# Sums in column streams, the order of two products, an earlier regrouping, and reciprocals in pieces, in a kernel of two attention layers

## The chip, the cores and the metric

The kernel runs on one core of a Trainium2 chip. Its engines work side by side, each through its own list of instructions in order: TensorE (PE) multiplies matrices, VectorE (DVE), ScalarE (ACT) and GpSimd (POOL) work on elements, and SyncE (SP) issues most transfers (DMAs). They wait for one another through semaphores. Matrix products land in PSUM, everything else lies in SBUF or in the chip's main memory. The metric is the time of one execution on the device in microseconds (us), as a median of runs. A profiled execution is a run of its own, with its own time.

## What is computed

The input is x, eight images of 512 channels and 32 x 32 = 1,024 tokens, all in f32. Two layers follow one another; each is `x = x + layer(groupnorm(x))`. Cut to what matters here:

```python
# layer 0, 8 heads of 64 channels; n = groupnorm of its input once more
q, k, v = split(qkv_w @ n + qkv_b)
a       = softmax(q.T @ k / 8) @ v          # per image and head, 1,024 x 1,024
out     = proj_w @ (n_in + a) + proj_b

# layer 1
q, k, v = w_q @ y, w_k @ y, w_v @ y
s       = einsum('gh,hqt->gqt', w_head, q.T @ k / 8)   # mixes the 8 heads
p       = softmax(s)
p       = (p - mean(p)) / sqrt(var(p) + eps) * gamma + beta   # per image and head
out     = (p @ v) as [tokens, channels] @ w_proj.T + b_proj
```

The softmax of both layers is done without its division: the kernel keeps exp(s), sums it over the keys, and multiplies the result of the values by the reciprocal of that sum.

## The kernel before

The order of every engine's instructions is the order of the program text; there is no planner. An `Agenda` holds small pieces of work under slot numbers, and the main loops call `run(slot)` at fixed places.

**Layer 0** goes image by image. The projections of q, k, v and the output each are seven products of half size in place of eight (`project0`). The attention of an image (`attention0`) is a loop over 64 steps: 8 groups (a pair of heads and half of the queries, 512 of them) times 8 blocks of 128 keys. A step has `scores` (four 64-row, 64-column matmuls in the four quadrants of the array, and then exp on ACT into a tile `e` of 128 x 2 x 512), and, one round later, `values` (four quadrant matmuls) and `sums` (DVE adds the `e` tiles of a group into `zacc`). When a group is through, the agenda gets three pieces of it: `totals` two steps on, `reciprocals` six on, `finish` ten on.

`totals` sums `zacc` over its partitions with a matmul by ones. Before, that is done in quadrants: for each half `a` of the partitions and each head `m` of the pair one matmul of 512 queries; the two halves lie in two PSUM tiles, ACT copies one into `row` and DVE the other, and two small DMAs spread a row over 128 partitions (`zc`). `reciprocals` adds the halves (`zs`), takes the reciprocal, and sends it through main memory (`zd`) to be broadcast over the partitions again (`rzb`); `finish` multiplies and adds into `xa`. In seven of the eight images the totals of the fifth group are followed on PE by a matmul of the next image's group statistics (L620), which waits for a small DVE copy (L618); and the totals of an image's last group come after the next image's k projection. In the last image nothing stands between them and the output projection.

**Layer 1** again goes image by image. `Projection` forms k, q and the output by seven products of quarters: `products` (eight matmul records of 512 columns each) and `leave` (what ACT or DVE does with the result). `run` takes them in `ORDER`. Products 3 and 4 are the last two: product 3 ends the quarter (0, 1), that is channels 0 to 255 and the later tokens; product 4 ends (1, 0), channels 256 to 511 and the earlier tokens. The k projections of all images but the first are placed by hand in the loop instead.

`Attention1` has 37 half-steps x. In `half_step(x)`, `scores` makes two score tiles (two of the four pairs of heads: pairs 0 and 1 when x is even, 2 and 3 when it is odd), which DVE or ACT copies to `raw`. A pair of half-steps fills the block t = x // 2 of `raw`. `regroup` then turns the block round with eight DMAs of 256 KB, r = 0 to 7, into one of the two halves of the buffer `re`, so that the heads lie along the partitions. Four half-steps after its scores, `mix` multiplies the block by the head weights (64 matmul records a mix, taken in `R_ORDER`), with exp on ACT; `squares`, `sum_e`, `sum_e2` and `values` follow one half-step later. In the steady state every mix and every values issues one regrouping DMA behind it. At the start (x up to 4) there is nothing to put them behind, and after the scores of x=1 and of x=3 all eight are issued at once.

`v_pair(b, i)` makes two blocks of 128 rows of v: sixteen matmul records, then one copy on ACT and one on DVE. Two of the four pairs of an image are made before its attention, two inside it. The weights of v lie in half of `re` at that time, in the space that the regrouping DMAs r = 0 to 3 of t=1 will write.

Every eight half-steps (a quarter `qb` of the queries) end with `totals(qb)`; two half-steps later `reciprocals` runs. It puts the broadcasts of `rzb` at the head of a list of pieces (`pieces`: also the loads of the next image and of weights), and `scores` sends one piece each time, behind its last matmul. `divide` multiplies by `rzb` six half-steps after the totals. For the last quarter of an image the broadcasts are issued at once.

PSUM has three tiles for scores, mixes and projections of layer 1 (`m_psum`), taken in turn; a matmul waits until the tile three back has been read.

Of the kernel before, what the change touches and what calls it, by code (L numbers as in the profile page):

```python
# [9 lines left out]
F32 = mybir.dt.float32  # L10
# [8 lines left out]
P = 128  # L19
# [448 lines left out]
def tile_two_attention_layers(  # L468
# [19 lines left out]
    nc = tc.nc  # L488
    B, C, T = x_d.shape
    H = w_head.shape[0]  # L490
    D = C // H
    NCC = C // P
    NT = T // P
    FB = 512
# [36 lines left out]
    ones = const_tile("ones", [P, P])  # L531
# [118 lines left out]
    with ExitStack() as l0:  # L650
# [9 lines left out]
        def small_psum(nm):  # L660
            return ps_a.tile([P, FB], F32, tag="small", name=nm)
# [308 lines left out]
        def attention0(b, agenda):  # L970
# [49 lines left out]

            def totals(g):

                z = [
                    ps_a.tile([P, FB], F32, tag="a0", name=f"z_{b}_{g}", bufs=2),
                    small_psum(f"z_{b}_{g}_1"),
                ]
                for a in range(2):
                    rows = slice(a * D, a * D + D)
                    for m in range(2):
                        nc.tensor.matmul(  # L1030
                            z[a][m * D : m * D + D], ones[rows, :D], zacc[g][rows, m],
                            start=True, stop=True,
                        )
                row = zpool.tile([P, 2, FB], F32, tag="row", name=f"row0_{b}_{g}", bufs=1)
                nc.scalar.copy(row[:, 0], z[0])
                nc.vector.tensor_copy(row[:, 1], z[1])
                zc[g] = stat.tile([P, 2, T // P], F32, tag="zc", name=f"zc_{b}_{g}")
                for a in range(2):
                    nc.sync.dma_start(out=zc[g][:, a], in_=row[0::D, a])

            def reciprocals(g):

                nc.vector.tensor_add(u[g][0], u[g][0], u[g][1])
                zs = stat.tile([P, T // P], F32, tag="zs", name=f"zs_{b}_{g}")
                nc.vector.tensor_add(zs, zc[g][:, 0], zc[g][:, 1])
                rz = stat.tile([P, T // P], F32, tag="rz0", name=f"rz_{b}_{g}")
                nc.vector.reciprocal(rz, zs)
                zd = dram.tile([2, FB], F32, tag=f"zd0_{b}_{g}", name=f"zd0_{b}_{g}")
# [100 lines left out]
    with ExitStack() as l1:  # L1149
# [144 lines left out]
                nc.vector.tensor_sub(t[:, i], x, y)  # L1294

        class Projection:
            ORDER = (1, 6, 2, 7, 5, 4, 3)

            def __init__(self, nm, key, n, t, finish, begin=None):

# [85 lines left out]
        def v_pair(b, i):  # L1386

            if i == 0:
                v_t[b] = kvpool.tile([P, NT, C], F32, tag="v", name=f"v1_{b}")
            ps = m_psum(f"pv1_{b}_{i}")  # L1390
            w = w_t["v", b]
            for m in range(2):
                for c in range(NCC):
                    nc.tensor.matmul(  # L1394
                        ps[:, m], y_t[b][:, c, ts(2 * i + m, P)], w[:, c],
                        start=(c == 0), stop=(c == NCC - 1),
                    )
            nc.scalar.copy(v_t[b][:, 2 * i], ps[:, 0])  # L1398
            nc.vector.tensor_copy(v_t[b][:, 2 * i + 1], ps[:, 1])  # L1399
# [158 lines left out]
        class Attention1:  # L1558
# [5 lines left out]
            def scores(self, x, i):  # L1564
# [15 lines left out]
                if x > MLAG:  # L1580
                    self.piece(last)
                if x % 2 and i == 1:
                    self.due = [(t, r) for r in R_ORDER]
                if x % 2 == 0 and i == 0:
                    self.raw[t] = rawpool.tile([P, H, 2, KB], F32, tag="raw", name=f"raw_{b}_{t}")
                dst = self.raw[t][:, 2 * hp : 2 * hp + 2]
# [133 lines left out]
            def reciprocals(self, qb, ag=None, x=None):  # L1720
# [7 lines left out]
                self.rzb = zpool.tile([P, T], F32, tag="rzb", name=f"rzb_{b}_{qb}")  # L1728
                rzb = self.rzb
                spread = [  # L1730
                    lambda two=two: nc.sync.dma_start(
                        out=rzb[two * D : two * D + D], in_=zd[two].partition_broadcast(D)
                    )
                    for two in range(2)
                ]
                if ag is None:
                    for fn in spread:
# [58 lines left out]
            def half_step(self, x, ag):  # L1796
# [23 lines left out]
                    self.scores(x, 1)  # L1820
                if 0 <= y < NX:
                    self.mix(y, 1)
                if x <= MLAG or x >= NX:
                    self.regroup(n=NR)
                if x >= NX:
# [28 lines left out]
        for b in range(B):  # L1854
            more = b + 1 < B
            a = Attention1(b)
            ag = Agenda()
            for i in range(NV):
                ag.at(1 + i, lambda i=i: v_pair(b, NV + i))
            free = (NX // 2 - 2 + b) % 2  # L1860
            if more:
                a.pieces += [lambda i=i: y_piece(b + 1, i) for i in range(4 * NCC)]
# [119 lines left out]
```

## Time and profile before

| what | value |
|---|---|
| median of 3 runs | 4345.27 us (4342.4 to 4345.67) |
| the profiled execution | 4355.81 us |
| its span, first to last instruction | 4353.9 us |
| TensorE clock granted | 0.995 of full speed |
| busy, share of the span: PE, DVE, ACT | 96%, 67%, 54% |
| one group's `totals` matmuls in layer 0 (64 groups) | 67.1 us busy in all |
| regrouping DMAs of 256 KB in layer 1 | 1,024 |
| broadcasts `rzb` in layer 1 | 64 of 256 KB |

In a line of a group, the first numbers are the busy time of all its instructions and the mean time of one in ns; behind the second bar stands how long the engine sat idle just before them, and what ended that. "64*64" is rows by columns of the array that a matmul takes up; each f32 matmul of the program gives two records. Matmuls overlap, so a record's length is longer than the distance to the next one. In a timeline the first number is the start in us from the span's start and the second the duration; in square brackets stands the idle time before. "issue" means that the engine waited for nothing that the profile shows. Idle time of an engine that isn't the bottleneck costs nothing.

### The profile page before, as it was taken

Reading aid. Unit: us, or ns where it says so; the run is one execution under the profiler, and the core shown is the slowest. Engines: PE = TensorE matmul, PEld = TensorE weight load, DVE = VectorE, ACT = ScalarE, POOL = GpSimd, SP = SyncE. Lnnn points to the kernel's source line nnn. Section 1 sums busy time; section 2 is a strip of 40 time slices with the busy share of each in tenths; the row PEclk is TensorE's granted clock in tenths of the full one; section 3 lists DMA queues with packets and bytes.
Section 4 is the critical chain, followed back from the end, with each engine's and each line's share of the span. In section 5 each row is a group of like instructions: output and inputs, shape, how many; then the busy total and the mean of one; then the engine's idle time right before and its main releaser. Section 6 shows DMA issues by size and latency. Waiting matters only on the chain.

```text
span 4353.9 us, 131477 instructions
## 1 busy us (share of the span) xinstructions
PE 4192.3 (96%) x58568; PEld 2243.2 (52%) x58568; DVE 2911.7 (67%) x3881; ACT 2329.9 (54%) x2730; POOL 53.3 (1%) x86
## 2 busy tenths in 40 slices
PE   7999999999999999799999999999999999999998
PEld 4353535353535353356466466466466466465565
DVE  4748484848484848458668668568577578577577
ACT  1717171717171716158368278277187287286385
POOL 0000000000000000000000000000000000000000
PEclk9999999999999999899999999999999999999999
DMA  4213131212121211257367377277286286375474
GB/s 145 77 54 101 50 104 49 79 49 79 52 76 54 74 49 43 87 140 191 123 166 183 105 187 180 97 195 189 81 202 172 90 206 158 114 199 141 135 175 136
DMA packets 260464, 521.21 MB, mean 120 GB/s; under 512 B 58992, under 2 KB 66544, under 8 KB 253232
## 3 DMA queue, kind: packets, MB, share of 16 engines
q1 hardware_dynamic: 255008, 509.92, 41.8%
q8 instruction: 461, 7.55, 0.8%
q0 software_dynamic: 2576, 0.69, 0.3%
q10 hardware_dynamic: 2304, 2.10, 0.2%
q14 instruction: 115, 0.94, 0.1%
HBM read 196.11 MB, written 46.92 MB: 56 GB/s over the span
## 4 chain that ended last, share of the span: by engine, by line
PE 84%; DVE 6%; DMA 5%; ACT 2%; issue 2%; SPq 1%; POOL 0%; DVEq 0%; ACTq 0%; POOLq 0%
PE a L1669 11%; PE s L1575 11%; PE m L1623 10%; PE s L982 8%; PE a L1008 8%; PE pk L1319 5%; PE pq L1319 4%; PE pp_p L856 4%; PE pv_p L856 4%; PE pv L1394 4%; PE pk_p L856 4%; PE pq_p L856 4%; PE pp L1319 3%; DMA re<-raw 2%; PE t L1700 2%
## 5 line engine op out<-in xcount | busy, mean ns | idle before, releaser
L1623 PEld LDWEIGHTS m<-wmix,re 64*64 64x64 f32 x32768 | 585.4, 135 | 141.9 <-issue 73.7
L1623 PE MATMUL m<-wmix,re 64*64 64x64 f32 x32768 | 602.1, 219 | 44.0 <-issue 34.9
L987 ACT ACTIVATE e<-s 128x1024 f32<-128x1024 f32 x512 | 497.4, 1026 | 235.4 <-PE s L982 235.4
L1629 ACT ACTIVATE e<-m 128x1024 f32<-128x1024 f32 x512 | 528.2, 1032 | 157.7 <-PE m L1623 154.2
L1647 DVE TENSOR_TENSOR z<-z,e 128x1024 f32<-128x1024 f32 x448 | 538.9, 1218 | 69.8 <-ACT e L1629 69.6
L1651 DVE TENSOR_TENSOR z<-z,e 128x1024 f32<-128x1024 f32 x448 | 534.9, 1219 | 74.6 <-ACT e L1640 74.4
L1669 PE MATMUL a<-e,v 128*64 128x256 f32 x4096 | 558.2, 392 | 27.5 <-ACT q L1691 20.9
L1575 PE MATMUL s<-k,q 64*64 64x256 f32 x8192 | 558.4, 388 | 6.2 <-DVE q L1431 4.6
L1590 ACT COPY raw<-s 128x1024 f32<-128x1024 f32 x368 | 372.7, 1015 | 284.4 <-PE s L1575 245.8
L982 PE MATMUL s<-q,k 64*64 64x512 f32 x4096 | 491.5, 594 | 2.3 <-ACT e L987 2.3
L995 DVE TENSOR_TENSOR zacc<-zacc,e 128x1024 f32<-128x1024 f32 x384 | 468.2, 1219 | 28.6 <-ACT e L987 3.9
L1008 PE MATMUL a<-e,v 64*64 64x512 f32 x4096 | 485.0, 589 | 0.0
L1640 ACT ACTIVATE e<-e 128x1024 f32<-128x1024 f32 x448 | 462.1, 1063 | 0.0
L1575 PEld LDWEIGHTS s<-k,q 64*64 64x64 f32 x8192 | 271.5, 132 | 274.5 <-issue 170.7
L1669 PEld LDWEIGHTS a<-e,v 128*64 128x64 f32 x4096 | 250.6, 136 | 155.0 <-issue 24.9
L1008 PEld LDWEIGHTS a<-e,v 64*64 64x64 f32 x4096 | 159.9, 133 | 281.2 <-issue 281.2
L982 PEld LDWEIGHTS s<-q,k 64*64 64x64 f32 x4096 | 156.2, 133 | 281.5 <-issue 257.7
L1588 DVE COPY raw<-s 128x1024 f32<-128x1024 f32 x144 | 176.1, 1223 | 96.3 <-PE s L1575 84.7
L1394 PE MATMUL pv<-re,y 128*128 128x512 f32 x512 | 227.6, 598 | 0.0
L1394 PEld LDWEIGHTS pv<-re,y 128*128 128x128 f32 x512 | 94.8, 190 | 120.1 <-issue 120.1
L1399 DVE COPY v<-pv 128x512 f32<-128x512 f32 x32 | 22.1, 689 | 149.4 <-ACT v L1398 149.4
L856 PE MATMUL pv_p<-left_v,tmp 128*128 128x256 f32 x512 | 115.1, 383 | 4.2 <-DVE tmp L885 4.2
(285 smaller groups left out, 4133.0 us busy)
## 6 DMA issues: line engine op xcount, KB each, us to landing
re<-raw SPq DMA_DIRECT2D x1024, 256.0 KB
left_q<-left_q SPq DMA_DIRECT2D x17, 1792.0 KB
left_p<-left_p SPq DMA_DIRECT2D x17, 1792.0 KB
left_k<-left_k SPq DMA_DIRECT2D x10, 1792.0 KB
x<-in_x_dram SPq DMA_DIRECT2D x32, 512.0 KB
rzb<-zd SPq DMA_DIRECT2D x128, 128.0 KB
x<-x SPq DMA_DIRECT2D x64, 256.0 KB
rzb<-zd SPq DMA_DIRECT2D x64, 256.0 KB
```

What stands on the lines that cost most here:

```text
L856: nc.tensor.matmul(out, st, mv, start=start, stop=(k == 1), skip_group_check=True)
L982: nc.tensor.matmul(ps[c * D : c * D + D, m], k[r, hp, k0 : k0 + D], q[r, hp, ts(f, FB)], start=True, stop=True,)
L987: nc.scalar.activation(e[i], ps, AF.Exp, scale=S0 * S0)
L1008: nc.tensor.matmul(acc[g][a][m * D : m * D + D], v[rows, kc, ts(2 * hp + m, D)], e[i][rows, m], start=(kc == 0), stop=(kc == NG - 1),)
L1319: nc.tensor.matmul(self.ps[m][:, i], w[:, left, k * HC + i * P : k * HC + i * P + P], right[:, k], start=(k == 0 and m != 2), stop=(k == 1 ...
L1394: nc.tensor.matmul(ps[:, m], y_t[b][:, c, ts(2 * i + m, P)], w[:, c], start=(c == 0), stop=(c == NCC - 1),)
L1575: last = nc.tensor.matmul(pv[c * D : c * D + D, m, j], qo_t[b][r, 2 * qb + j, hp, ts(c, D)], k_t[b][r, hp, ts(kb, KB)], start=True, stop=True,
L1623: last = nc.tensor.matmul(ps[c * D : c * D + D, a, ts(r, D)], self.re[t, r][rows, j, k0 : k0 + D], wmix[rows].rearrange("p g i -> p (g i)" ...
L1629: nc.scalar.activation(self.e[y][:, j], ps.rearrange("p a c -> p (a c)"), AF.Exp)
L1647: nc.vector.tensor_add(self.z[:, j], self.z[:, j], self.e[y][:, j])
L1651: nc.vector.tensor_add(self.z2[:, j], self.z2[:, j], self.e2[j])
L1669: last = nc.tensor.matmul(self.acc[w][two * D : two * D + D, s].rearrange("p (c i) -> p c i", i=Q8), v_t[b][:, kc, ts(g, D)], e[:, g], sta ...
```

## The change

Four edits, in two layers:

1. `totals` of layer 0 uses the whole height of the array: four matmuls of 128 rows and 32 columns side by side, each for one quarter of the 2 x 512 sums, 256 elements long. The result lies in one PSUM tile of 256 columns; ACT alone copies it, one DMA fetches it, and no halves are left to add.
2. `ORDER` ends with product 4 instead of product 3.
3. The second v pair inside an attention moves from the end of half-step 2 to half-step 3, behind its scores and in front of its regrouping; and the regrouping of t=1 takes r = 4 to 7 first.
4. `rzb` of layer 1 is broadcast by four DMAs of 32 partitions instead of two of 64.

```diff
             def totals(g):
-                z = [
-                    ps_a.tile([P, FB], F32, tag="a0", name=f"z_{b}_{g}", bufs=2),
-                    small_psum(f"z_{b}_{g}_1"),
-                ]
-                for a in range(2):
-                    rows = slice(a * D, a * D + D)
-                    for m in range(2):
-                        nc.tensor.matmul(
-                            z[a][m * D : m * D + D], ones[rows, :D], zacc[g][rows, m],
-                            start=True, stop=True,
-                        )
-                row = zpool.tile([P, 2, FB], F32, tag="row", name=f"row0_{b}_{g}", bufs=1)
-                nc.scalar.copy(row[:, 0], z[0])
-                nc.vector.tensor_copy(row[:, 1], z[1])
-                zc[g] = stat.tile([P, 2, T // P], F32, tag="zc", name=f"zc_{b}_{g}")
-                for a in range(2):
-                    nc.sync.dma_start(out=zc[g][:, a], in_=row[0::D, a])
+                HB = FB // 2
+                z = ps_a.tile([P, FB], F32, tag="a0", name=f"z_{b}_{g}", bufs=2)[:, :HB]
+                for c in range(4):
+                    nc.tensor.matmul(
+                        z[c * 32 : c * 32 + 32], ones[:, :32], zacc[g][:, c // 2, ts(c % 2, HB)],
+                        start=True, stop=True, tile_position=(0, c * 32),
+                    )
+                row = zpool.tile([P, HB], F32, tag="row", name=f"row0_{b}_{g}")
+                nc.scalar.copy(row, z)
+                zc[g] = stat.tile([P, T // P], F32, tag="zc", name=f"zc_{b}_{g}")
+                nc.sync.dma_start(out=zc[g], in_=row[0::32])
             def reciprocals(g):
                 nc.vector.tensor_add(u[g][0], u[g][0], u[g][1])
-                zs = stat.tile([P, T // P], F32, tag="zs", name=f"zs_{b}_{g}")
-                nc.vector.tensor_add(zs, zc[g][:, 0], zc[g][:, 1])
+                zs = zc[g]
...
         class Projection:
-            ORDER = (1, 6, 2, 7, 5, 4, 3)
+            ORDER = (1, 6, 2, 7, 5, 3, 4)
...
                 if x % 2 and i == 1:
-                    self.due = [(t, r) for r in R_ORDER]
+                    order = (4, 5, 6, 7, 0, 1, 2, 3) if t == 1 else R_ORDER
+                    self.due = [(t, r) for r in order]
...
                 spread = [
-                    lambda two=two: nc.sync.dma_start(
-                        out=rzb[two * D : two * D + D], in_=zd[two].partition_broadcast(D)
+                    lambda i=i: nc.sync.dma_start(
+                        out=rzb[ts(i, 32)], in_=zd[i // 2].partition_broadcast(32)
                     )
-                    for two in range(2)
+                    for i in range(4)
                 ]
...
                 if 0 <= y < NX:
                     self.mix(y, 1)
+                ag.run(x - 0.75)
                 if x <= MLAG or x >= NX:
                     self.regroup(n=NR)
...
-            for i in range(NV):
-                ag.at(1 + i, lambda i=i: v_pair(b, NV + i))
+            for i, slot in enumerate((1, 3 - 0.75)):
+                ag.at(slot, lambda i=i: v_pair(b, NV + i))
```

## The prediction

> **What bounds the kernel now.** I read the page's shares first, then the chain, then the groups of TensorE (PE), then what PE waited for, and last the timeline at the places that the change touches.
>
> ```profile
> span 4353.9 us, 131477 instructions
> PE 4192.3 (96%) x58568; PEld 2243.2 (52%) x58568; DVE 2911.7 (67%) x3881; ACT 2329.9 (54%) x2730; POOL 53.3 (1%) x86
> PE 84%; DVE 6%; DMA 5%; ACT 2%; issue 2%; SPq 1%; POOL 0%; DVEq 0%; ACTq 0%; POOLq 0%
> ```
>
> PE is the bound nearly everywhere: 96% busy, 84% of the chain. So an edit pays only by taking PE work away, or one of PE's few idle stretches. Two groups of sums, of layer 0 and of layer 1:
>
> ```profile
> L1700 PE MATMUL t<-z,ones 128*32 128x512 f32 x512 | 70.0, 599 | 5.5 <-DVE z L1651 5.5
> L1030 PE MATMUL z<-zacc,ones 64*64 64x512 f32 x512 | 67.1, 593 | 2.3 <-DVE zacc L995 1.4
> ```
>
> L1700 already runs in the form that the change gives to L1030: 128 rows by 32 columns. Each program matmul shows as two records (two passes of f32). What PE waited for (total, times, longest):
>
> ```profile
> PE m L1623 <- issue: 34.9, 51, 2.3
> PE pm L620 <- DVE gs_m L618: 21.3, 8, 10.4
> PE m L1623 <- DMA re<-raw: 7.9, 14, 1.1
> PE pp_p L856 <- DVE tmp_xa L836: 7.5, 1, 7.5
> PE s L1575 <- DVE q L1431: 4.6, 8, 0.6
> ```
>
> The timeline of one image of layer 1 shows the regrouping of t=1 as it is issued, the stall at x=6 that it causes, and the end of the q projection:
>
> ```profile
> 2524.87 7.33 SPq L1599 DMA_DIRECT2D re<-raw  x8
> 2536.79 0.34 PE L1623 MATMUL m<-wmix,re 64*64 64x64 f32 x8 [0.48 <-DMA re<-raw]
> 2537.78 0.53 PE L1623 MATMUL m<-wmix,re 64*64 64x64 f32 x8 [0.65 <-DMA re<-raw]
> ...
> 2500.95 2.04 DVE L1431 TENSOR_TENSOR q<-pq,sum 128x512 f32<-128x512 f32 x2 [1.39 <-PE pq L1319]
> 2502.07 3.79 PE L1575 MATMUL s<-k,q 64*64 64x256 f32 x60 [0.57 <-DVE q L1431]
> 2503.19 1.22 DVE L1588 COPY raw<-s 128x1024 f32<-128x1024 f32 x1 [0.20 <-PE s L1575]
> ```
>
> **What the Trainium skill says.** "TensorEngine Tiling (Array Packing)", Key Properties: changing the tiling mode drains the array. The trace agrees: from one round of 64*64 matmuls of 512 to the next is 409 ns, to a 128-row form 519 (+110); from 128-row forms of 512 back to 64*64 it is 522 against 429 (+93). "TensorE: Matmul & The Clock Gate", Measured speedup vs the span model: tiles side by side take one matmul plus some ns a tile. The trace agrees: the four streams of L1700 start 7 ns apart, and its rounds follow every 429 ns, like one full 128*128 matmul. "Runtime: NRT & Kernel Launch", Instruction fetch mechanics: instructions come in 16 KiB blocks, mostly hidden. Here only in part: queue q8 moved 461 such blocks, and each long "issue" idle of PE ends 2.6 to 3.1 us after a block's transfer began. No page prices the moved regrouping.
>
> **Layer 0, sums in four streams (64 groups).** Before: two rounds of four 64*64 matmuls of 512 elements; from the first to the next work of PE is 858 ns, with no drain (all neighbours are 64*64). After: two rounds of four 128*32 matmuls of 256 elements. A full matmul of 256 elements repeats every 216 ns (L856), and 256-element 128-row forms reach the next form after 309 ns (L1669 to L1575: 209 and a drain). So 216 + 20 (stagger) + 309 = 545 ns, plus 110 for the drain on entry: 655, a gain of 203 ns.
> - 49 groups between values and scores: 49 x 0.203 = 9.9 us.
> - 7 groups followed by the statistics matmul L620: PE there waits for DVE L618, which stands behind the copy L1036. L1036 to L618 is 0.60 us start to start; the copy is dropped, so PE gets 0.60: 7 x 0.60 = 4.2 us. (DVE's own wait for the rzb DMA ahead of it stays, so not more.)
> - 7 groups after the k projection: 1.02 us to the next work, entered behind a wait that hides the entry drain; after: 545 ns. 7 x 0.47 = 3.3 us.
> - The last group's chain is exposed, as the timeline shows:
>
> ```profile
> 1752.26 0.68 DVE L1036 COPY row<-z 128x512 f32<-128x512 f32 x1
> 1755.08 0.20 DVE L1047 RECIPROCAL rz<-zs 128x8 f32<-128x8 f32 x1
> 1764.16 2.07 PE L856 MATMUL pp_p<-tmp_xa,left_p 128*128 128x512 f32 x2 [7.45 <-DVE tmp_xa L836]
> ```
>
> The second zc DMA was issued at 1752.97, after DVE's row copy, which stood behind the finish of the group before; the reciprocal followed at 1755.08. With one copy on ACT the DMA can go at about 1749.7 and land by 1751.6; then DVE's finish (to 1752.35) and the add of u (0.69) are last: reciprocal at 1753.05, 2.0 us earlier. The rest of the chain is unchanged: 2.0 us.
>
> Sum 19.4 us. ACT's shorter copy, 64 fewer zc DMAs on SP, and the small adds of zs lie beside PE and are costed at nothing; PE covers them, and uncovered they would be gains.
>
> **Order of the last two products.** In the q projection the scores of x=0 no longer need the last product (heads 4 to 7), so the 0.57 us wait goes, 4.6 us in eight images. What is late next: DVE still has two adds of 1.04 us for that product and then the raw copy of the first scores (1.22) before the fourth scores get their PSUM buffer (three of them). That raw copy began only 0.20 us after the adds. So the fourth scores start 0.2 us earlier, not 0.57: 8 x 0.2 = 1.6 us (bounds 0 and 4.6). Layer 1's first k projection and seven output projections do the same work in the other order, behind other products: nothing. If that cover went, a 1.2 us DVE add each.
>
> **Second v pair in front of the regrouping of t=1.** PE's work up to mix(0) is the same, only the second v pair now stands behind the scores of x=2 and 3 instead of between them; forms change equally often. The raw block of t=1 is ready one v pair (16 matmuls x 429 ns, 6.9 us) earlier. r=4..7, which don't overlap the v weights, are issued then, at about T-5.7 (T = start of the scores of x=4); r=0..3 wait on SP for the v pair and go at T+0.7 to T+3.7. Nothing else is queued behind them on SP until x=5. Before: issued T+1.3 to T+8.6, packets until about T+14. mix(2) needs them from T+10.5; after, the last lands by about T+8. The fifth mix of each image takes 1.49 to 3.51 us where 0.89 is normal; of that excess 8.0 us in all were released by the regrouping. All of it goes: 8.0 us. The raw buffer that DVE and ACT refill at x=6 is free earlier too; that wait was hidden by PE's work from other buffers.
>
> Fetch stalls at x=5 and 6 add up to 12.8 us (8.2 and 4.6); other half-steps of that kind have 0.5 to 1.6. The burst that shared the DMA engines moves ahead to the v pair, which needs few instructions; but without DMA waits PE also meets its fetches sooner. Bounds +8 (the whole gain is lost again) and -10; I take -3.
>
> **Reciprocals in four pieces.** Two DMAs of 256 KB become four of 128 KB. One piece goes behind each scores, so x=16 and 17 instead of 16 alone (24 and 25 likewise); the divide at the end of x=18 has a half-step of 5.9 us, and such a piece of layer 0 landed about 3 us after its issue (1757.25 to 1760.29). SP issues 64 more of them in all, and 64 fewer zc. Other pieces (y, left weights) go one half-step later and have slack until x=24. At an image's end the four are issued at once, past them the xs and left_q loads by about 0.5 us; the divide began at 2449.20 while both old DMAs had ended their packets by about 2447: hidden with 2 us. In the last image the divide does wait for them (4330.23) with PE just behind: -0.3 to +0.5, I take 0. Mid-image fetch stalls gather at x=16 to 18 (13.7 us) and 24 to 26 (11.3), right after the old DMAs; a normal half-step would leave about 7 of these 25. Shorter bursts on twice as many half-steps: from -12 to +6; I take -2.
>
> **Sum.** 19.4 + 1.6 + 8.0 + 3 + 2 = 34 us, from one profiled execution of 4355.81 us (span 4353.9). It lies 10.5 us above the median of 4345.27, a fixed part that I carry over: 4345.3 - 34 = 4311 us.
>
> **Rivals.**
> 1. Fetch stalls take back what the DMA waits gave, and the pieces bring nothing: 19.4 + 1.6 + about 2 = 23 us, 4322. For it: the stalls are as large as the waits at that very place; against: they lie where bursts lie. 0.17.
> 2. Bursts were the cause of most: fetch stalls at x=5, 6, 16 to 18, 24 to 26 fall to normal: 29 + 9 + 13 = 51 us, 4294. For: where they gather; against: x=4 and 5 are dense in matmuls whatever DMA does. 0.08.
> 3. The column streams don't do what they say: entry and exit drains eat them (another 0.2 us a group, 13 us): about 4325 to 4335. L1700 speaks against it, though no 256-element form of it is in the trace. 0.06.
> 4. Slower: the four streams of 32 columns run one after another. Eight passes of 216 ns plus 0.2 of drains are 1.93 us a group, 1.07 more than now: 64 x 1.07 = 68 us lost against 20 won elsewhere, 4393. It decides from 1.2 us a group on. Against it stand the four starts of L1700 within 20 ns. 0.04.
>
> **How the numbers follow.** The main case, 4304 to 4318, gets 0.62; a remainder of 0.03 is within 0.2% (8.7 us, about what can be told from no change). The range leaves out rival 4, most of 2 and half of 3: 4298 to 4325. Faster 0.93, same 0.03, slower 0.04.
>
> **What would show it.** In the profile after: the z group at 38 us or less with 128*32 and 256 elements, and PE's next start some 0.55 us after it; L620's wait down by some 4 us; the wait of PE s on DVE q gone, with a new one for DVE raw; PE m on DMA re near 2; issue idle of m below 34.9. Wrong would be a z group at its old busy time, issue idle above 42, or a wait for rzb ahead of the divide.

## The result, and the profile after

| | kernel before | changed kernel |
|---|---|---|
| median | 4344.5 us (4342.4 to 4345.67, 4 runs) | 4286.02 us (4284.02 to 4287.71, 4 runs) |
| the profiled execution, its span | 4355.81 us, 4353.9 | 4284.02 us, 4282.2 |
| ratio of the medians, 95% interval | | 0.9866 [0.9849, 0.9883] |

The change gains 58.5 us where 34 was forecast. The time lies below the range (4298 to 4325), close to rival 2 (4294). A second measurement of both kernels gave 4293.43 against 4346.11 us, ratio 0.9871 [0.9851, 0.9891]. The profiled execution of before was some 11 us above its median. I therefore use a second profile of the kernel before as well (4345.96 us, span 4344.2); between it and the profile after lie 62.0 us.

The page of the changed kernel, shares and chain:

```profile
span 4282.2 us, 131340 instructions
PE 4163.5 (97%) x58568; PEld 2214.3 (52%) x58568; DVE 2862.9 (67%) x3753; ACT 2316.0 (54%) x2730; POOL 53.4 (1%) x86
PE 89%; DVE 5%; DMA 3%; ACT 2%; issue 1%; SPq 0%; POOL 0%; DVEq 0%; ACTq 0%; POOLq 0%
```

PE has 28.8 us less work in its records, and the chain runs through PE for 89% instead of 84% of the span: the shares of DMA (5% to 3%) and issue (2% to 1%) went down with it. The two groups of sums, of layer 1 and of layer 0:

```profile
L1696 PE MATMUL t<-z,ones 128*32 128x512 f32 x512 | 69.8, 599 | 5.4 <-DVE z L1647 5.4
L1027 PE MATMUL z<-zacc,ones 128*32 128x256 f32 x512 | 40.9, 391 | 0.9
```

The group of layer 0 has the new form, and 40.9 instead of 67.1 us. What PE waited for:

```profile
PE m L1619 <- issue: 15.7, 29, 1.4
PE pm L620 <- DVE gs_m L618: 10.6, 2, 10.4
...
PE pp_p L856 <- DVE tmp_xa L836: 4.3, 1, 4.3
...
PE s L1569 <- DVE q L1425: 2.9, 8, 0.4
```

Two of these fell far more than the forecast had it. L620's wait fell from 21.3 to 10.6, and 10.4 of the rest is one wait at the start of layer 1: the seven waits inside layer 0 went from 10.9 to 0.2. The issue idle of the mixes fell from 34.9 to 15.7. The timeline of the image whose start was shown of before:

```profile
2464.55 2.08 DVE L1425 TENSOR_TENSOR q<-pq,sum 128x512 f32<-128x512 f32 x2 [1.39 <-PE pq L1313]
2466.77 2.14 PE L1569 MATMUL s<-k,q 64*64 64x256 f32 x32 [0.37 <-DVE q L1425]
2467.92 1.22 DVE L1584 COPY raw<-s 128x1024 f32<-128x1024 f32 x1 [0.17 <-PE s L1569]
...
2480.70 8.25 SPq L1595 DMA_DIRECT2D re<-raw  x8
```

The first scores begin at 2464.44, while DVE still adds; the wait for q now sits 2.33 us later, in front of the third scores, with 0.37 instead of 0.57 us. The eight regrouping DMAs of t=1 are issued from 5.9 us before the first scores of x=4 (at 2486.59) to 2.4 us after; in the image of before they went from 1.3 to 8.6 us after these scores. No mix of this image waits for one at x=6. And the end of layer 0:

```profile
1724.23 0.39 ACT L1032 COPY row<-z 128x256 f32<-128x256 f32 x1
...
1726.86 0.20 DVE L1041 RECIPROCAL rz<-zc 128x8 f32<-128x8 f32 x1
...
1735.84 1.56 PE L856 MATMUL pp_p<-tmp_xa,left_p 128*128 128x512 f32 x2 [4.31 <-DVE tmp_xa L836]
```

**Where the time came from.** Cut by stages, in us. Layer 1's half-steps are measured from one half-step's first score matmul to the next one's, summed over the eight images. In the six half-steps of the lower two rows a half-step without any stall takes 5.94 us, which makes 142.5 for three of them in eight images:

| stage | before | before, second profile | after |
|---|---|---|---|
| start of the span to layer 1's first scores | 1869.6 | 1868.6 | 1840.7 |
| x=0 to 3 | 181.9 | 181.9 | 177.1 |
| x=4 to 6 | 149.0 | 148.7 | 134.4 |
| x=16 to 18 | 158.4 | 157.5 | 147.6 |
| x=24 to 26 | 155.5 | 153.4 | 147.5 |

Layer 0 gives 28.9, the order 4.8, the moved v pair 14.6, and the half-steps with the broadcasts 18.8 (15.8 against the second profile). The forecast had 19.4, 1.6, 11 and 2 for them.

### The profile page after: what moved, and what is told of

Read it like the earlier page. It is cut to its first block, busy times and chain, and to the rows that moved or that the text cites. A ratio compares the mean times of both kernels' runs of the same rounds, so it can differ in the third digit from the quotient of the medians.

```text
span 4282.2 us, 131340 instructions
## 1 busy us (share of the span) xinstructions
PE 4163.5 (97%) x58568; PEld 2214.3 (52%) x58568; DVE 2862.9 (67%) x3753; ACT 2316.0 (54%) x2730; POOL 53.4 (1%) x86
## 4 chain that ended last, share of the span: by engine, by line
PE 89%; DVE 5%; DMA 3%; ACT 2%; issue 1%; SPq 0%; POOL 0%; DVEq 0%; ACTq 0%; POOLq 0%
PE a L1665 11%; PE s L1569 11%; PE m L1619 11%; PE s L982 10%; PE a L1008 10%; PE pk L1313 5%; PE pq L1313 4%; PE pp_p L856 4%; PE pv_p L856 4%; PE pv L1388 4%; PE pk_p L856 4%; PE pq_p L856 4%; PE pp L1313 3%; PE t L1696 2%; DMA re<-raw 1%
## 5 line engine op out<-in xcount | busy, mean ns | idle before, releaser
L1619 PE MATMUL m<-wmix,re 64*64 64x64 f32 x32768 | 592.0, 219 | 20.8 <-issue 15.7
L1008 PEld LDWEIGHTS a<-e,v 64*64 64x64 f32 x4096 | 156.7, 133 | 282.8 <-issue 282.8
```

What stands on the lines that cost most here:

```text
L1008: nc.tensor.matmul(acc[g][a][m * D : m * D + D], v[rows, kc, ts(2 * hp + m, D)], e[i][rows, m], start=(kc == 0), stop=(kc == NG - 1),)
L1619: last = nc.tensor.matmul(ps[c * D : c * D + D, a, ts(r, D)], self.re[t, r][rows, j, k0 : k0 + D], wmix[rows].rearrange("p g i -> p (g i)" ...
```

## The experiments

Two things were to be explained: why layer 0 gave nine us more than was forecast for it, and whether the fetch stalls at x=4 to 6, 16 to 18 and 24 to 26 hang on the bursts of DMAs, as rival 2 has it, or lie where they like. All kernels start from the kernel before unless said otherwise. Where a run has a ratio, it is against runs of the kernel before on the same chip; their median lay between 4345 and 4352 us from chip to chip, so ratios are to be compared and not times.

A fetch stall here is idle time of PE that the profile calls "issue". That PE then waits for a block of instructions is read from the transfers of these blocks, which come some 9 us apart: the 35 issue waits over 0.5 us in the kernel before all end 2.3 to 3.1 us after a block's transfer began, and the 15 in the changed kernel 2.2 to 3.0 us after. There are two measures of a stall. The view of waits counts from the modelled end of the matmul before; the prediction counted from start to start, which gives some 0.2 us more for each stall.

### Each edit alone

**The sums alone** (`totals` and `reciprocals` of layer 0 as in the diff above).

> The kernel before with the sums of layer 0 in four streams alone. Theory after the two traces: layer 0 is 28.9 us shorter in the changed kernel, and all of that is this edit: 49 groups x 0.18 us (858 to 569 ns, and 110 more on entry), 7 groups x 0.46, 10.7 us because the waits of L620 go nearly to zero, 5 us at the layer's end. So 25 to 31 us faster, layer 1 unchanged within 5 us. The prediction's sum gave 19.4. Rival: part of the gain in layer 0 was chance of the one profiled execution of before; then 15 to 20 us.

4319.04 us, ratio 0.9924 [0.9908, 0.9941], which is 33 us (26 to 40). The trace puts layer 1's first scores at 1841.46 us where before had 1869.61 and 1868.61: 27 to 28 us. L620's wait is 11.5, that of the output projection 4.3, as in the full change. So layer 0's gain is this edit's, within the scatter of layer 0 (see the sum at the end of the terms below).

**The order alone.**

```diff
-            ORDER = (1, 6, 2, 7, 5, 4, 3)
+            ORDER = (1, 6, 2, 7, 5, 3, 4)
```

> The kernel before with the new ORDER alone. From the traces: from the first scores of an image to the v pair 4.94 us before and 4.40 after, eight images: 4.3 us faster. The prediction's step gave 1.6 (DVE is next). In the trace: 4.4 us from the first scores to the v pair, a wait for DVE q of 0.37 us that now stands before the third scores.

4348.64 us, ratio 0.9993 [0.9985, 1.0]: too small to be told by the times. In the trace the half-steps x=0 take 18.6 instead of 23.3 us in eight images (4.7 less), and those of x=1 73.0 after 72.8: the gain is kept.

**The v pair alone**, with both halves of the edit (place, and r = 4 to 7 first).

> The kernel before with the second v pair in front of the regrouping of t=1 and that regrouping's order r = 4 to 7 first, alone. Theory: the DMA waits at x=6 go (8.0 us), fetch stalls at x=4 to 6 fall from 13.5 to about 9 us: 10 to 14 us faster. Rival (fetch stalls take the gain back): 0 to 5 us faster, with issue stalls at x=5 and 6 above 15 us.

4332.2 us, ratio 0.9954 [0.9937, 0.997], 20 us (13 to 27). x=4 to 6 take 134.3 us, 14.5 less than in the two profiles of before; x=16 to 18 (158.1) and 24 to 26 (153.0) are unchanged. The waits of PE have for the mixes' issue idle, 34.9 before:

```profile
PE m L1625 <- issue: 25.8, 38, 1.7
```

The waits for a regrouping at x=6 are gone.

**The pieces alone** (four broadcasts of 32 partitions, 128 KB each).

> The kernel before with the broadcasts of rzb in four pieces alone. Theory: the broadcasts of 64 partitions delay PE's instruction blocks; issue stalls at x=16 to 18 and 24 to 26 fall from 25 us to below 8: 12 to 18 us faster. Rival 1 (the stalls fell because the steadier regrouping of the other edit changed the phase of everything behind it, or by chance): within 4 us of before. Prediction's step: 2 us.

4336.93 us, ratio 0.9958 [0.9944, 0.9972], 18 us (12 to 24). x=16 to 18 fall to 147.8 and x=24 to 26 to 150.9, while x=4 to 6 stay (151.8). The forecast had 2 us for it. The gain is just where the broadcasts are. The profiled execution as a whole has a span only 5 us shorter than the second profile of before (4339.2 against 4344.2 us), so it is these half-steps and the median that count here.

### Is it a property of the places, or chance?

**The kernel before once more**, unchanged.

> The kernel before once more, unchanged, for a second profile on the chip of these runs. If the stalls on instruction blocks belong to the places and not to one execution, they gather again at x=5 and 6, 17 and 25, with 33 to 45 us of issue idle in all and a wait of L620 of 10 to 11 us beside the 10.4 at the start of layer 1. If they are chance, the places change.

4345.96 us. The stalls gather at the same places again: 148.7, 157.5 and 153.4 us. The 42.6 us of issue idle in the first profile are 40.0 here. So the places are the kernel's. The sums of these two profiles agree to about 2 us, and those of all kernels with the same broadcasts (table below) to 3 or 4; one place in one image can't be compared.

### Layer 0: what holds L620

The forecast gave L620 the 0.60 us of DVE's row copy. That would be a matter of DVE's queue alone, so I took this copy off DVE and left the matmuls as they were:

```diff
-                nc.vector.tensor_copy(row[:, 1], z[1])
+                nc.scalar.copy(row[:, 1], z[1])
```

> The kernel before (sums in quadrants), but ACT makes both copies of the sums; DVE's copy L1036 is gone. Theory (a loop: DVE's copy stands behind the wait for rzb, delays the second zc DMA, so the sum zs, so the reciprocal, so the next rzb): the wait of L620 falls from 21 to 11 us, the layer's last stall from 7.5 to about 5, layer 0 is 12 to 18 us shorter, with the 49 other groups at 858 ns as before. Rival (the prediction's step: only the copy's own 0.6 us goes): layer 0 is 4 to 6 us shorter and L620 waits 16 to 17 us.

4341.98 us, ratio 0.9982 [0.9975, 0.9989], 8 us; the trace has 8 to 9 us in layer 0. From the sums to L620 it is 2.20 us in each of the seven places, together 15.4, after 18.25 before (2.04 to 3.62 each). L620 waits 8.1 us there, so 18.5 with the one at the start of layer 1: neither the 11 of the theory nor the 16 to 17 of its rival. Only the last stall of the layer came as the theory had it, with 5.4 us. The queue alone is not what holds L620. The timeline of one of these places, first of before, then of this kernel (lines that don't matter here are left out):

```profile
182.82 0.69 DVE L1068 TENSOR_TENSOR u<-u,rzb 128x512 f32<-128x512 f32 x1 [1.31 <-DMA rzb<-zd]
182.86 1.04 PE L1030 MATMUL z<-zacc,ones 64*64 64x512 f32 x8
...
183.54 0.69 DVE L1070 TENSOR_TENSOR xa<-xa,u 128x512 f32<-128x512 f32 x1
...
184.15 0.68 DVE L1036 COPY row<-z 128x512 f32<-128x512 f32 x1
184.75 0.16 DVE L618 COPY gs_m<-mv 128x4 f32<-128x4 f32 x1
185.06 0.36 PE L620 MATMUL pm<-gs_m,gavg 128*128 128x4 f32 x2 [1.16 <-DVE gs_m L618]
```

```profile
183.39 0.16 DVE L618 COPY gs_m<-mv 128x4 f32<-128x4 f32 x1
183.46 1.04 PE L1030 MATMUL z<-zacc,ones 64*64 64x512 f32 x8
184.53 0.58 ACT L1035 COPY row<-z 128x512 f32<-128x512 f32 x1 [1.34 <-PE z L1030]
185.01 0.59 ACT L1036 COPY row<-z 128x512 f32<-128x512 f32 x1
185.66 0.39 PE L620 MATMUL pm<-gs_m,gavg 128*128 128x4 f32 x2 [1.16 <-ACT row L1036]
```

L618 now comes before the sums, but L620 waits all the same: for ACT's copy of the second half. `z[1]` and L620's result are both made by `small_psum`, and that pool has one buffer for the name "small". So before, L620 stood behind two things at once: the PSUM buffer that the copy read, and DVE's queue, in which L618 came after the copy. With one of them gone the other is about as late. (Part of the 2.20 us is this edit's own: ACT's second copy ends 2.14 us after the start of the sums, DVE's copy in the place shown ended after 1.97.)

What the copy stood behind in DVE's queue can be read as well. In five of the seven places it begins right after `finish` of the group before (L1068 and L1070), which had waited for the broadcast of that group's reciprocals; only in the other two did it wait for the sums, 1.13 us after their start. And these broadcasts come earlier when the copy is gone, since a group's copy stands at the head of the chain to its own broadcast. In the seven places DVE's wait for the broadcast ended between 0.65 us before the start of the sums and 1.38 us after it; with both copies on ACT between 1.72 and 0.08 us before it; in the changed kernel at least 0.76 us before, where there is such a wait at all. In the whole of layer 0, of before, with both copies on ACT, and changed:

```profile
DVE u L1068 <- DMA rzb<-zd: 93.9, 44, 5.9
DVE u L1068 <- DMA rzb<-zd: 67.7, 29, 5.8
DVE u L1062 <- DMA rzb<-zd: 55.2, 22, 6.5
```

The change takes both away, the place in DVE's queue and the shared buffer:

```profile
183.34 0.64 PE L1027 MATMUL z<-zacc,ones 128*32 128x256 f32 x8
183.91 0.38 PE L620 MATMUL pm<-gs_m,gavg 128*128 128x4 f32 x2
184.05 0.37 ACT L1032 COPY row<-z 128x256 f32<-128x256 f32 x1 [1.08 <-PE z L1027]
```

L620 follows after 0.57 us with no wait, before anyone has read the sums. To see the two apart, **the changed kernel with half of the copy on DVE**: the buffer is free, the copy is back in front of L618.

```diff
-                nc.scalar.copy(row, z)
+                nc.scalar.copy(row[:, : HB // 2], z[:, : HB // 2])
+                nc.vector.tensor_copy(row[:, HB // 2 :], z[:, HB // 2 :])
```

> The changed kernel, but DVE again copies a part (half) of the sums of layer 0, so that its copy and the zc DMA stand behind its wait for rzb; the PSUM tile that L620 uses stays free. If DVE's place in line is what L620 waited for, its wait comes back: 7 to 11 us beside the 10.4 at the start of layer 1, and the layer's last stall grows by 2 us or more. If it was the PSUM tile alone, L620 waits below 2 us.

4294.35 us in one run. From the sums to L620 the seven places take 10.47 us: 18.25 before, 4.21 in the changed kernel. L620's wait and the wait at the end of layer 0:

```profile
PE pm L620 <- DVE gs_m L618: 16.4, 8, 10.4
PE pp_p L856 <- DVE tmp_xa L836: 5.6, 1, 5.6
```

So of 14.0 us at L620, 7.8 come with the streams in one buffer and shorter copies, and 6.3 with DVE being left out, as far as one profile tells. At the end of layer 0 DVE's copy costs 2.7 us: from the last values to the work behind the wait it is 15.91 us here and 13.25 in the changed kernel (of the difference 1.3 lie in the wait shown, 5.6 against 4.3).

### The broadcasts: how many at once, how large

The pieces changed three things: a DMA's size, its partitions, and how many half-steps the broadcasts take. **The old two broadcasts, one half-step apart:**

```diff
-                    ag.at(x + 1, lambda: self.pieces.__setitem__(slice(0, 0), spread))
+                    for i in range(2):
+                        ag.at(
+                            x + 1 + i,
+                            lambda i=i: self.pieces.__setitem__(slice(0, 0), spread[i : i + 1]),
+                        )
```

> The kernel before, with the two broadcasts of 64 partitions issued in two half-steps (x=16 and 17, 24 and 25) instead of both in one. If it is the two together that delay the instruction blocks, the stalls at x=17 and 25 fall to normal (x=17: 49 us over eight images where before has 53 to 56; 25: 49 where it has 55 to 57). If one broadcast of 64 is enough, they stay at half or move to x=18 and 26: the sum of x=16 to 18 stays above 154 us.

4343.1 us, ratio 0.9985 [0.9977, 0.9993], 6.5 us. x=16 to 18 keep 157.8 us, with the excess moved towards x=18 (51.1, 52.3, 54.4); x=24 to 26 fall to 149.6. Spreading helps at the second place, as much as pieces do, and not at the first.

**Four broadcasts of 64 partitions and half of the columns**: again 128 KB each, but in the other direction.

```diff
-                    lambda two=two: nc.sync.dma_start(
-                        out=rzb[two * D : two * D + D], in_=zd[two].partition_broadcast(D)
+                    lambda two=two, f=f: nc.sync.dma_start(
+                        out=rzb[two * D : two * D + D, ts(f, FB)],
+                        in_=zd[two, ts(f, FB)].partition_broadcast(D),
                     )
                     for two in range(2)
+                    for f in range(2)
```

> The kernel before with four broadcasts of 64 partitions x 512 elements (packets of 2 KB, 128 KB each) instead of two of 64 x 1,024. If the size of a piece counts (128 KB instead of 256), x=16 to 18 and 24 to 26 fall as with four pieces of 32 partitions: x=17 and 25 near 49 us. If it is the number of partitions (descriptors) of a broadcast, they stay at 53 to 57.

4334.96 us, ratio 0.9966 [0.9954, 0.9979], 15 us. x=16 to 18 150.3, x=24 to 26 148.5: the same relief as with 32 partitions. So the shape of a piece doesn't count.

Whether its size does is not shown. In these half-steps the list of pieces also sends loads of 128 KB, one DMA for each scores, so the edits also change how much is issued in a half-step. Beside the regroupings, which are the same in all of them, the queue issues in seven of the eight images (the last has no such loads here):

| kernel | KB issued at x=16, 17, 18 | x=16 to 18, us | KB at x=24, 25, 26 | x=24 to 26, us |
|---|---|---|---|---|
| before | 512, 256, 256 | 158.4, 157.5 | 512, 0, 0 | 155.5, 153.4 |
| broadcasts apart | 384, 384, 256 | 157.8 | 256, 256, 0 | 149.6 |
| pieces alone | 256, 256, 256 | 147.8 | 256, 256, 0 | 150.9 |
| halves of columns | 256, 256, 256 | 150.3 | 256, 256, 0 | 148.5 |

The amount in a half-step fits all of it, and the size of a piece does not: two broadcasts of 256 KB are no burden at x=24 and 25, where nothing else is sent (one profile, but the 6.5 us of the times fit the fall at this one place). At x=16 to 18 they are, but there each shares its half-step with a load. No run tells the two apart at x=16 to 18; four pieces of 128 KB in one half-step would.

**The changed kernel with eight pieces of 64 KB** (16 partitions each), so two in a half-step again but over four half-steps, and the divide two half-steps later for the first two quarters of an image, so that it need not wait for the last piece:

```diff
-                        out=rzb[ts(i, 32)], in_=zd[i // 2].partition_broadcast(32)
+                        out=rzb[ts(i, 16)], in_=zd[i // 4].partition_broadcast(16)
                     )
-                    for i in range(4)
+                    for i in range(8)
...
-                            ag.at(x + 6, lambda: self.divide(qb))
+                            ag.at(x + (6 if qb == NQB - 2 else 8), lambda: self.divide(qb))
```

> The changed kernel with the broadcasts of rzb in eight pieces of 16 partitions (64 KB) over four half-steps, and the divide two half-steps later for the first two quarters of an image. If smaller pieces still help: 3 to 6 us faster than the changed kernel. If 128 KB is small enough already: the same within 3 us; eight issues at an image's end cost at most 1 us each.

4297.43 us, ratio 0.9892 [0.9874, 0.991]. Beside it on the same chip **the changed kernel itself**:

> The changed kernel unchanged, beside the next one: 1.1 to 1.6% faster than before, near 4286 us. Issue idle of PE near 19 us, x=17 and 25 near 49 us, if the first profile was no chance.

4293.43 us, 0.9871 [0.9851, 0.9891]. The six half-steps take 297.5 with eight pieces and 294.8 with four. Half the size, and half the amount in a half-step, once more brings nothing that can be seen, and the two intervals overlap.

### The v pair: place and order

**The v pair moved, the regrouping in its old order** (r = 0, 4, 1, 5, 2, 6, 3, 7; r=0 waits on SP for the v pair, and the others behind it).

```diff
                     self.mix(y, 1)
+                ag.run(x - 0.75)
...
-            for i in range(NV):
-                ag.at(1 + i, lambda i=i: v_pair(b, NV + i))
+            for i, slot in enumerate((1, 3 - 0.75)):
+                ag.at(slot, lambda i=i: v_pair(b, NV + i))
```

> The kernel before with the second v pair in front of the regrouping of t=1, but the regrouping in its old order (r=0 first). SP then waits at r=0 for the v pair, so all eight DMAs go after it, at T+0.7 to T+8 instead of T+1.3 to T+8.6. If the new order is needed, x=4 to 6 take 145 to 149 us over eight images, as before (149), with DMA waits of m of 5 us or more at x=6. If the earlier place alone is enough, they take 134 to 138, as with both (134.3).

4338.1 us in one run. The DMA wait at x=6 is gone here too (the mixes wait for a regrouping for 1.9 us in all), but x=4 to 6 take 140.1 us; the six profiles with both halves of the edit have 134.3 to 135.8. The difference is fetch: from start to start, issue idle at x=5 is 10.5 us in eight images, 5.2 in the changed kernel. So the place takes the DMA wait away, and the order some 5 us of fetch stalls, as far as one profile tells. The 140.1 lies between the two forecasts.

### Do the gains add up?

The four ratios alone make 33 + 3 + 20 + 18 = 74 us, the whole change 56 to 58. Either the intervals cover that, or edits that both relieve fetch share one gain. So I undid each of the two inside the changed kernel. First **two broadcasts of 256 KB**, the rest as changed:

> The changed kernel with the broadcasts of layer 1 undone to two of 256 KB; the other three edits stay. Theory A (the edits add up: the size of a broadcast piece decides at x=16 to 18 and 24 to 26, whatever else is changed): these six half-steps go back from 295 us in eight images to about 312, issue idle of PE rises by some 15 us, and the kernel loses about 15 us against the changed one: ratio to the kernel before about 0.990 to 0.991. Theory B (PE's fetch stalls are shared out: what is taken away in one place comes back in another, so the separate gains overlap): the six half-steps get longer, but others get shorter, the loss is at most 6 us, and the ratio stays at 0.987 to 0.988.

4303.57 us (5 runs), ratio 0.9903 [0.9889, 0.9916]: 14 to 16 us lost against the ratios of the changed kernel. The six half-steps go back to 308.3 us, and x=4 to 6 stay at 135.3; the amount in a half-step has gone back here together with the size of a broadcast. The waits of PE have 9 us more issue idle in the mixes than the changed kernel's 15.7:

```profile
PE m L1619 <- issue: 24.7, 37, 1.6
```

Then **the old place of the v pair and the old order**, the rest as changed:

> The changed kernel with the second v pair and the regrouping of t=1 put back as they were; the other three edits stay. Theory A (the edits add up): the half-steps x=4 to 6 go back from 134 us in eight images to about 149, the DMA wait at x=6 returns with some 8 us and the fetch stalls there with some 6, and the kernel loses 14 to 20 us against the changed one: ratio to the kernel before about 0.9905 to 0.992. Theory B (the gains overlap): the wait for the DMA returns with 8 us, but the fetch stalls fall elsewhere or hide behind that wait; loss at most 9 us, ratio 0.989 or less.

4305.62 us (5 runs), ratio 0.9902 [0.9887, 0.9916]: 13 to 16 us lost. x=4 to 6 take 150.6 us again, x=16 to 18 and 24 to 26 stay short (148.6 and 147.4). In the waits of PE the mixes wait for the regrouping as before (7.9 there, 3.9 in the changed kernel; at x=6 alone 5.5 us here, 5.8 and 4.1 in the two profiles of before, none in the changed kernel):

```profile
PE m L1618 <- DMA re<-raw: 7.5, 14, 0.9
```

Both follow theory A, the second a little under its range: each edit is worth about the same inside the change as alone, within the intervals, and each moves its own half-steps only. That the four ratios make 74 is then left to their intervals (each of the larger three is 6 to 7 us either way). All four are also taken against the same runs of before, with the highest median of all (4352.36 us), so an error in these counts four times; that it does is not shown. The sums of the traces make 61.5, as worked out below.

All profiles side by side, in us, eight images together:

| kernel | broadcasts | x=4 to 6 | x=16 to 18 | x=24 to 26 | issue idle of PE |
|---|---|---|---|---|---|
| before | 2 x 256 KB | 149.0 | 158.4 | 155.5 | 42.6 |
| before, second profile | 2 x 256 | 148.7 | 157.5 | 153.4 | 40.0 |
| sums alone | 2 x 256 | 149.8 | 154.5 | 153.4 | 34.8 |
| order alone | 2 x 256 | 150.5 | 155.4 | 152.7 | 36.0 |
| both row copies on ACT | 2 x 256 | 148.8 | 158.9 | 154.6 | 39.2 |
| v pair moved, old order | 2 x 256 | 140.1 | 155.4 | 154.3 | 40.7 |
| v pair alone | 2 x 256 | 134.3 | 158.1 | 153.0 | 33.0 |
| changed, two broadcasts | 2 x 256 | 135.3 | 155.5 | 152.8 | 31.0 |
| broadcasts apart | 2 x 256 | 147.5 | 157.8 | 149.6 | 36.9 |
| pieces alone | 4 x 128 | 151.8 | 147.8 | 150.9 | 32.4 |
| halves of columns | 4 x 128 | 148.4 | 150.3 | 148.5 | 34.0 |
| changed, old v pair | 4 x 128 | 150.6 | 148.6 | 147.4 | 29.3 |
| changed | 4 x 128 | 134.4 | 147.6 | 147.5 | 19.4 |
| changed, again | 4 x 128 | 135.8 | 149.5 | 145.3 | 25.6 |
| changed, half of the copy on DVE | 4 x 128 | 134.5 | 148.2 | 146.3 | 20.6 |
| changed, eight pieces | 8 x 64 | 134.6 | 149.1 | 148.4 | 27.7 |

Down the column of x=16 to 18, the nine kernels with 256 KB have 154.5 to 158.9 and the seven with less 147.6 to 150.3: no overlap, whatever else they do. The eight of the first group that issue both at once have means of 156.7 and 153.7 us; the seven have 148.7 and 147.8. The pieces are worth 8.0 + 5.9 = 14 us.

## Why the prediction was wrong

Its direction and its list of places were right. Five terms of its sum were too small, two a little too large, one was right.

- **Streams, 49 x 203 ns = 9.9 us: 179 ns, 8.8 us.** From the start of the sums to PE's next start it is 569 ns after 858 before, and the drain at the entry is 110 ns (519 against 409), as forecast. The forecast took 545: the two rounds follow after 240 ns, not 216. The same 24 ns could be seen in the kernel before: L1700's second round starts 453 ns after its first, and only the later ones follow every 429.
- **Seven groups after the k projection, 3.3 us: 2.2.** The next work is reached after some 0.71 us and not 0.545.
- **L620, 4.2 us: 13.3.** This is the largest miss in layer 0. The seven places go from 18.25 to 4.21 us, less 0.8 for the drain at their entry. The step priced the copy that stands in front of L618 by its distance, 0.60 us, and said that DVE's wait for the rzb DMA stays, "so not more". It did not stay: the copy itself had made the broadcasts late. In two of the places the copy waited for the sums, so L618 stood behind PE's own work. And L620 waited for the buffer that the copy read, which the step left out. Without all of these, L620 waits 0.2 us in seven places. The experiments on L620 show the queue and the buffer.
- **The end of layer 0, 2.0 us: 4.3.** From the last values to the work behind the wait it is 13.25 us after 17.55. From the sums on it is 2.9 us: the reciprocal comes 3.75 us after their start, before 6.53. The other 1.4 lie ahead of the sums, which now start 0.5 us after the last values and before 1.9: DVE is not as far behind without its row copies (with both copies on ACT the sums start 0.4 us after the last values, too). The forecast looked only behind the sums.
- **The order, 1.6 us: 4.3** from the first scores to the v pair (4.40 us an image after 4.94). The wait for q did not go, as the forecast said it would; it moved to the third scores with 0.37 us. The new wait for a raw copy did come, but it costs less than was taken: the raw copy itself starts 2.09 us after the first scores, before 2.34.
- **DMA waits at x=6, 8.0 us: 8.0**, from start to start (5.8 in the view of waits). All gone; they come back when the edit is undone. The four DMAs that wait for the v weights go earlier than was forecast, from 2.5 us before the first scores of x=4 to 2.4 after, and not from 0.7 to 3.7 after: two of them are issued while the v pair still runs.
- **Fetch at x=4 to 6, 3 us: about 6.6** (14.6 in all less the 8.0). Inside its bounds. From start to start, issue idle at x=5 and 6 fell from 12.8 to 5.7 us, and 2.9 came up at x=4; the other 2.4 us have no name in the trace.
- **Fetch at x=16 to 18 and 24 to 26, 2 us: 14.** The largest miss of all, just beyond its bound of 12. The step said that "a normal half-step would leave about 7 of these 25" and then took a tenth of the difference. The table shows that nearly all of it hangs on how the broadcasts are cut and spread.

The terms as measured: 8.8 + 2.2 + 13.3 + 4.3 + 4.3 + 8.0 + 6.6 + 14 = 61.5 us, beside 62.0 between the second profile of before and the profile after, and 58.5 between the medians. That it meets the 62.0 so closely is chance. The eight profiles with the old sums and copies of layer 0 reach layer 1's first scores at 1865.8 to 1870.5 us, the six with the new ones at 1840.3 to 1845.3: 26.6 us between the means, where the four terms of layer 0 make 28.6.

Of the signs that the prediction named, PE's next start after the sums (0.57 us) and the issue idle of the mixes (15.7) came. The group of sums took 40.9 us and not 38 or less; the wait on q shrank to 2.9 and did not go; the mixes' wait for a regrouping fell to 3.9, not near 2. None of its signs of being wrong came: a wait for rzb ahead of a divide stands in the last image (7.6 us), but it did before as well (6.9).

**The rivals.** Rival 2 (bursts are the cause of most fetch stalls, 4294) was the right one for layer 1: it wanted 22 us of fetch stalls at these places, and 20.6 went. It had the chance of 0.08 because x=4 and 5 are dense in matmuls; there 8 us of stalls indeed stay, but at x=16 to 26 they don't. It still lay 8 us too high, for layer 0. Rival 1 (DMA waits turn into fetch stalls) falls with the v pair alone: x=4 to 6 lost 14.5 us where the DMA waits were 8. Rivals 3 and 4 fall with the 569 ns.

**The Trainium skill** says in "Runtime: NRT & Kernel Launch", Instruction fetch mechanics, that fetches are mostly hidden. The traces say how large the other part is here: 40 to 43 us of issue idle before and 19 to 26 after, for the same 461 blocks.

**What stays open.** Why two broadcasts of 256 KB in one half-step hold up a fetch and four halves over two half-steps don't, and whether the size of a piece has a part in it beside the amount in a half-step. The regrouping DMAs have 256 KB each too, and run all the time. In these half-steps a 4 KB packet of a broadcast took 220 and 254 ns (medians of x=16 to 18 and of x=24 to 26) before and 159 in every kernel that sends 32 partitions at a time; with the two broadcasts a half-step apart it took 173 and 179. A block itself took about as long in both (medians of 1.17 and 1.19 us before, 1.13 and 1.06 after). So the block's own transfer hardly lasts longer; it starts later. Counted from the same instruction of PE, the 31 blocks of x=16 to 18 begin on average 0.3 to 0.5 us earlier with four pieces (either shape, the rest as before) than in the two profiles of before, and 0.1 to 0.2 us earlier with the broadcasts apart; the 32 blocks of x=24 to 26 begin 0.2 to 0.3 us earlier in all three kernels. Which packets a block stands behind isn't to be seen in the trace. Regroupings in smaller DMAs were not tried.

## What to carry to other kernels

Before you price an instruction that is taken out of a queue, ask what that instruction itself waited for and which buffer it held: here a 0.6 us copy stood behind DVE's wait for a broadcast, made the next broadcast late in its turn, and held the only PSUM buffer of the next matmul, and it took the removal of both, the place in the queue and the hold on the buffer, to gain 2 us a place. Stalls that gather behind certain DMAs in every image are a cost of these DMAs, even where no semaphore joins them; sum them by half-step over all images, and try to send less of them at a time. What such an edit is worth should be read from its own half-steps, since the whole time moves by 10 us from run to run.

## What was not expected of the hardware

- Two broadcasts of 256 KB in one half-step against four of 128 KB over two, the same bytes from the same source: 14 us of PE's time in 48 half-steps, with either way of halving; eight of 64 KB over four half-steps are no better. The blocks of instructions begin later, and hardly take longer.
- The second round of four streams of 128 rows and 32 columns, 256 elements each, starts 240 ns after the first; full-width matmuls of 256 elements follow every 216 ns. With 512 elements the second round of streams starts after 453 ns, the later ones follow every 429.
- The issue idle of PE differs by 6 us between two profiles of one kernel (19.4 and 25.6), at changing places.
